# Feed-forward in eighths of a group, with the down product formed unit tile by unit tile

## The chip, the cores and the metric

The kernel runs on one core of a Trainium2 chip. The metric is the device time of one execution in microseconds; the time before is the median of three runs.

## The reference

Input is `x` of 64 batches with 256 tokens of 256 features, and `adj`, a 0/1 matrix for each batch. Two layers follow one another: each adds a graph part and then a feed-forward part to `x`, each behind a layer norm. The first layer's feed-forward is an LSTM of 256 steps. Only the last part, the second layer's feed-forward, is touched by the change:

```python
def blk_fn(xx):                                   # max-plus product, then two envelopes of 8 lines
    t = jnp.max(xx[:, None, :] + Wt[None, :, :], axis=-1) + bt
    z = t[:, :, None]
    cvx = jnp.max(z * sl_cvx[None] + of_cvx[None], axis=-1)
    ccv = jnp.min(z * sl_ccv[None] + of_ccv[None], axis=-1)
    return s * cvx + (1.0 - s) * ccv
trop = jax.lax.map(blk_fn, xb).reshape(T, FFN)
classical = jax.nn.gelu(xf @ Wc + bc, approximate=False)
g = jax.nn.sigmoid(xf @ Wg + bg)
fused = g * trop + (1.0 - g) * classical
out = fused @ Wd + bd
```

There are 16384 tokens, 256 features (`D`) and 1024 units (`FFN`, `FF`).

## The kernel before

A framework records the instructions and sets their order on each engine and the buffers of each pool at build time; within an engine the order is then fixed. `tc.issue_after(ins)` puts instructions behind another one on the same engine.

The kernel has stages in order of time: the first graph part, the LSTM, a short preparation, the second graph part, and from about 2660 us on the second feed-forward. The second graph part leaves for each token the normalised features, a copy in which only the features that can win the max-plus maximum stand, and the residual. It also leaves how many features can win.

The feed-forward sorts the tokens by that number in four blocks (`sorted_block`) and works on 128 tiles of 128 tokens, four tiles to a group (`GT` = 4), so 32 groups (`NGR`). Tiles at one place of a block take the same number of ranks, `RANKS`, from 40 down to 2; a group mixes tiles so that each has about the same sum. The 1024 units are 8 unit tiles (`NF` = 8), sorted by the number of hinges that their envelopes need, `HRANKS = [6, 3, 2, 2, 1, 1, 1, 0]`. A group passes through these pieces:

- `ask` (line 1274): GpSimd's indirect DMA gathers a tile's payload.
- `pick` (1282): VectorE finds the largest features, 8 at a time, with their numbers; TensorE transposes the tile and ScalarE copies it to `xr`.
- `maxplus` (1301): for each rank an indirect DMA of GpSimd brings one row of `wT_d` for each token (`row`, 128 x 1024, 10 buffers). The first rank of a tile goes through ScalarE (line 1313), which makes `acc`; all others are VectorE's step of line 1316, add and maximum.
- `classical` (1318): TensorE forms the gate and the GELU products of two unit tiles (line 1331), ScalarE applies the functions (line 1338), with a table load between the two.
- `fuse` (1340): TensorE transposes `acc` into `pa` (line 1348), ScalarE and VectorE form the hinges from it (`fused_hinges`, lines 1193 to 1203), and the result is a part of `fu`, which holds all 8 unit tiles of the group.
- `down` (1358): with the whole `fu` there, TensorE forms the down product in `po` for two tiles at a time (lines 1209 and 1211: the bias as a matmul of one row, then 8 products for each tile), and VectorE adds it to the residual (line 1218).
- `ask_rest` (1353) and `give_back` (1366): GpSimd gathers the residual and scatters the output.

The loop of line 1385 interleaves the pieces of neighbouring groups in quarters: while group g takes its rows, g - 1 is fused, g + 1 is asked for and picked, and g - 2 gets its down product. GpSimd's queue carries all indirect DMAs in this order; SP's and ScalarE's queues carry none in the group loop.

Of the kernel before, what the change touches and what calls it, by code (L numbers as in the profile page):

```python
# [2 lines left out]

# [6 lines left out]
F32 = mybir.dt.float32  # L10
# [5 lines left out]
AF = mybir.ActivationFunctionType  # L16
ALU = mybir.AluOpType
# [4 lines left out]
P = 128  # L22
# [35 lines left out]
def kernel(ctx: ExitStack, tc: tile.TileContext, a: dict, out: bass.AP):  # L58
# [16 lines left out]
    nc = tc.nc  # L75
    B, N, D = a["x"].shape
    H = D
    K = D // P
    NC = N // P
    FF = a["Wt"].shape[0]  # L80
    NF = FF // P
# [7 lines left out]
    ident = const.tile([P, P], F32, name="ident")  # L89
# [8 lines left out]
    ones = const.tile([P, N], F32, name="ones")  # L98
# [200 lines left out]
    with tc.tile_pool(name="b0", bufs=1) as wp:  # L299
        bias = wp.tile([6, 4 * P], F32, name="bias")  # L300
        part = wp.tile([6, 4 * P], F32, name="part")
# [220 lines left out]
    with (  # L522
# [345 lines left out]
        for k in range(HINGES):  # L868
            sc, of, sg = (prm_u[:, :, 4 + 3 * k + n] for n in range(3))
# [235 lines left out]
    CH = 512  # L1105
# [3 lines left out]
    class FeedForward:  # L1109
# [80 lines left out]
        def fused_hinges(self, f, pa, cl, gg, out, tag):  # L1190

            v = self.p4.tile([P, CH], F32, name=f"v_{tag}_{f}", tag="cvx")
            nc.scalar.activation(  # L1193
                v, pa, AF.Identity, bias=prm[:, f, 1:2], scale=prm[:, f, 0:1]
            )
            for k in range(HRANKS[f]):
                sc, of, sg = (prm[:, f, 4 + 3 * k + n : 5 + 3 * k + n] for n in range(3))
                u = self.u4.tile([P, CH], F32, name=f"u_{tag}_{f}_{k}", tag="u")
                nc.scalar.activation(u, pa, AF.Relu, bias=of, scale=sc)  # L1199
                nc.vector.scalar_tensor_tensor(v, u, sg, v, ALU.mult, ALU.add)  # L1200
            nc.vector.tensor_tensor(v, v, cl, ALU.subtract)
            nc.vector.tensor_tensor(v, v, gg, ALU.mult)  # L1202
            nc.vector.tensor_tensor(out, v, cl, ALU.add)  # L1203

        def down(self, fused, res, tag):

            po = self.ps_o.tile([P, NC, D], F32, name=f"po_{tag}", tag="po")
            for c in range(NC):
                nc.tensor.matmul(po[:, c, :], ones[0:1, :P], self.b_d, start=True, stop=False)
                for f in range(NF):  # L1210
                    nc.tensor.matmul(  # L1211
                        po[:, c, :],
                        fused(f, c),
                        self.w_d[:, f, :],
                        start=False,
                        stop=(f == NF - 1),
                    )
                nc.vector.tensor_tensor(res[c], res[c], po[:, c, :], ALU.add)

    with (  # L1220
        tc.tile_pool(name="w4", bufs=1) as wp,
        tc.tile_pool(name="s4", bufs=1) as sp,
        tc.tile_pool(name="pay4", bufs=5) as payp,
        tc.tile_pool(name="xr4", bufs=3) as xrp,
        tc.tile_pool(name="res4", bufs=7) as resp,
        tc.tile_pool(name="tk4", bufs=8) as tkp,
        tc.tile_pool(name="row4", bufs=10) as rowp,
        tc.tile_pool(name="acc4", bufs=8) as accp,
        tc.tile_pool(name="p4", bufs=2) as p4,
        tc.tile_pool(name="u4", bufs=3) as u4,  # L1230
        tc.tile_pool(name="cg4", bufs=2) as cgp,
        tc.tile_pool(name="fu4", bufs=1) as fup,
        tc.tile_pool(name="ps_c4", bufs=6, space=PSUM) as ps_c,
        tc.tile_pool(name="ps_o4", bufs=2, space=PSUM) as ps_o,
    ):
# [12 lines left out]
            nc.vector.tensor_copy(perm[blk][:, 1, :], order)  # L1248

        ff = FeedForward(wp, (p4, u4, cgp, ps_c, ps_o), True)  # L1250

        def place(i, of):
            j = i % NB
            return bass.IndirectOffsetOnAxis(ap=perm[i // NB][:, of, j : j + 1], axis=0)


        GT = CH // P
# [6 lines left out]
        class Group:  # L1264


            def __init__(self, g):
                self.g = g
                blk, m = divmod(g, GPB)
                self.tiles = [blk * NB + j for j in mixed[m]]  # L1270
                self.pay, self.val, self.num, self.acc, self.res = {}, {}, {}, {}, {}
                self.ranks = [(q, r) for q, i in enumerate(self.tiles) for r in range(RANKS[i % NB])]

            def ask(self, q):
# [26 lines left out]
            def maxplus(self, part):  # L1301

                n = len(self.ranks)
                for q, r in self.ranks[part * n // GT : (part + 1) * n // GT]:
                    i = self.tiles[q]
                    row = rowp.tile([P, FF], F32, name=f"row_{i}_{r}", tag="row")
                    nc.gpsimd.indirect_dma_start(  # L1307
                        row, None, wT_d, bass.IndirectOffsetOnAxis(ap=self.num[q][:, r : r + 1], axis=0)
                    )
                    v = self.val[q][:, r : r + 1]  # L1310
                    if r == 0:
                        acc = self.acc[q] = accp.tile([P, FF], F32, name=f"acc_{i}", tag="acc")
                        nc.scalar.activation(acc, row, AF.Identity, bias=v)  # L1313
                    else:
                        acc = self.acc[q]
                        nc.vector.scalar_tensor_tensor(acc, row, v, acc, ALU.add, ALU.max)  # L1316

            def classical(self, part):

                self.cg = {}  # L1320
                kinds = [
                    ("cl", ff.w_c, ff.col["bc"], AF.Gelu),
                    ("gg", ff.w_gt, ff.col["bg"], AF.Sigmoid),
                ]
                for n, wgt, bias, func in kinds[:: -1 if part % 2 else 1]:
                    res = self.cg[n] = cgp.tile([P, FQ, CH], F32, name=f"{n}_{self.g}_{part}", tag=n)
                    for e in range(FQ):
                        f = part * FQ + e
                        pc = ps_c.tile([P, CH], F32, name=f"pc_{n}_{self.g}_{f}", tag="pc")
                        for k in range(K):  # L1330
                            nc.tensor.matmul(  # L1331
                                pc,
                                wgt[:, k, f * P : (f + 1) * P],
                                self.xr[:, k, :],
                                start=(k == 0),
                                stop=(k == K - 1),
                            )
                        nc.scalar.activation(res[:, e, :], pc, func, bias=bias[:, f : f + 1])  # L1338

            def fuse(self, part):  # L1340
                g = self.g
                if part == 0:
                    self.fu = fup.tile([P, NF, CH], F32, name=f"fu_{g}", tag="fu")
                for e in range(FQ):
                    f = part * FQ + e
                    pa = ps_c.tile([P, CH], F32, name=f"pa_{g}_{f}", tag="pc")
                    for q in range(GT):
                        nc.tensor.transpose(  # L1348
                            pa[:, q * P : (q + 1) * P], self.acc[q][:, f * P : (f + 1) * P], ident
                        )  # L1350
                    ff.fused_hinges(f, pa, self.cg["cl"][:, e, :], self.cg["gg"][:, e, :], self.fu[:, f, :], g)

            def ask_rest(self, q):
                i = self.tiles[q]
                res = self.res[q] = resp.tile([P, D], F32, name=f"res_{i}", tag="res")
                nc.gpsimd.indirect_dma_start(res, None, res_d[i // NB], place(i, 0))

            def down(self, part):
                q0 = part * NC
                ff.down(  # L1360
                    lambda f, c: self.fu[:, f, (q0 + c) * P : (q0 + c + 1) * P],
                    [self.res[q0 + c] for c in range(NC)],
                    f"{self.g}_{part}",
                )

            def give_back(self, q):
                nc.gpsimd.indirect_dma_start(  # L1367
# [5 lines left out]
        FQ = NF // GT  # L1373
        NGR = NT // GT
        groups = [Group(g) for g in range(NGR)]

        def each(g, piece, *args):
            if 0 <= g < NGR:
                getattr(groups[g], piece)(*args)
# [3 lines left out]
            groups[0].ask(q)  # L1383
            groups[0].pick(q)
        for g in range(NGR + 2):
            for q in range(GT):
                if q == 0:
                    for part in range(GT // NC):
                        each(g - 2, "down", part)
                    each(g - 1, "classical", 0)  # L1390
                each(g + 1, "ask", q)
                each(g, "maxplus", q)
                each(g - 1, "fuse", q)
                if q + 1 < GT:
                    each(g - 1, "classical", q + 1)
                each(g + 1, "pick", q)
                each(g - 1, "ask_rest", q)
                each(g - 2, "give_back", q)
            if g % GPB == GPB - 2 and g + 2 < NGR:
                sorted_block((g + 2) // GPB)  # L1400

# [19 lines left out]
    with tc.If(bad > 0):  # L1421
        with (
# [9 lines left out]
            ff = FeedForward(wp, (p4, u4, cgp, ps_c, ps_o), False)  # L1432
# [6 lines left out]
            with tc.For_i(0, NBLK, 1) as blk:  # L1439

                acc = [accp.tile([P, TOK], F32, name=f"accg{f}", tag=f"acc{f}") for f in range(NF)]
# [26 lines left out]
                for ch in range(NCH):  # L1468
# [3 lines left out]
                    cl, gg = ff.classical(xr, f"g{ch}")  # L1472
# [83 lines left out]
```

## Time and profile before

| | us |
|---|---|
| median of three runs (5421.66 to 5444.79) | 5427.94 |
| profiled execution, time | 5416.64 |
| profiled execution, span | 5414.8 |
| feed-forward, group loop (2690 to 5350) | 2660 |
| VectorE busy in it | 2315.19 |
| GpSimd busy in it | 1917.03 |
| ScalarE busy in it | 1263.52 |
| TensorE busy in it | 1819.53 |

A page of a profile shows one execution. It has the busy time of each engine, the span in 40 slices with a digit for the busy share of each, the groups of instructions by line (count, busy time, mean of one, idle time before them and what ended it), and the DMA issues. DVE is VectorE, ACT is ScalarE, POOL is GpSimd, PE is TensorE. The issuing of an instruction by GpSimd's sequencer is not counted as busy. Where a wait's releaser is "remote" or "issue", the trace names no instruction that ended it.

### The profile page before, as it was taken

The page shows a single profiled execution, that of the slowest core. Times are in us where ns is not written, and L with a number is a line of the kernel's source. Part 1 is how long each engine was busy: PE and PEld are TensorE (multiplying, and loading weights), DVE is VectorE, ACT ScalarE, POOL GpSimd, SP SyncE. Part 2 cuts the span into 40 slices and gives each one's busy share as a digit, 9 for nine tenths or more (in the row PEclk, how much of TensorE's full clock was granted, in tenths as well). Part 3 has the DMA queues.
Part 4 walks back from the last instruction along what each step waited for, and adds up shares of the span by engine and source line. Part 5 has one row for each costly group of instructions (what it writes and reads, how often), then busy time and mean ns, then how long its engine had stood idle before and what let it go on. Part 6 is the DMA issues. An engine that isn't in the chain of part 4 may idle for free. (4 is left out here: it accounts for less than half of the span.)

```text
span 5414.8 us, 58603 instructions
## 1 busy us (share of the span) xinstructions
PE 4203.9 (78%) x17787; PEld 2348.7 (43%) x17788; DVE 4183.2 (77%) x9223; ACT 2276.6 (42%) x4245; POOL 2546.2 (47%) x2739
## 2 busy tenths in 40 slices
PE   6999979999999978888547677577675776666777
PEld 4666623333333336666424334344343443334444
DVE  5777776555555568888788799888898888897997
ACT  2555512222222225555434444354444544345555
POOL 1333310000000025555488667777667676677764
PEclk8999989999999989999768888788887888888889
DMA  4322212111111124444388776777767777677774
GB/s 107 94 84 85 72 38 73 46 28 28 28 28 28 28 83 143 143 138 139 131 301 270 258 252 229 262 250 264 251 231 261 252 270 248 220 259 261 268 258 140
DMA packets 454032, 886.60 MB, mean 164 GB/s; under 512 B 60232, under 2 KB 285004, under 8 KB 453708
## 3 DMA queue, kind: packets, MB, share of 16 engines
q0 software_dynamic: 192448, 685.96, 37.9%
q1 hardware_dynamic: 253476, 193.64, 12.5%
q10 hardware_dynamic: 7784, 3.17, 0.3%
q8 instruction: 143, 2.34, 0.2%
q14 instruction: 181, 1.48, 0.1%
HBM read 773.34 MB, written 110.26 MB: 163 GB/s over the span
## 5 line engine op out<-in xcount | busy, mean ns | idle before, releaser
L1307 POOL DMA_INDIRECT row<-wT_d,num x1172 | 1421.4, 1213 | 565.6 <-issue 277.9
L1316 DVE SCALAR_TENSOR_TENSOR acc<-row,val,acc 128x1024 f32<-128x1024 f32 x1044 | 1314.1, 1279 | 166.0 <-DMA row<-wT_d,num 161.3
L1211 PE MATMUL po<-w_d,fu 128*128 128x256 f32 x2048 | 593.5, 436 | 106.8 <-DVE fu L1203 100.0
L1331 PE MATMUL pc_gg<-xr,w_gt 128*128 128x512 f32 x1024 | 538.0, 667 | 97.2 <-ACT u L1199 64.2
L568 PE MATMUL pg<-w_hh,hT 128*64 128x512 f32 x2040 | 501.5, 613 | 91.6 <-DVE hT L695 91.5
L949 POOL TENSOR_TENSOR adjT<-adjT,ident 128x128 f32<-128x128 f32 x128 | 61.5, 502 | 1020.3 <-PE pg L568 991.6
L1211 PEld LDWEIGHTS po<-w_d,fu 128*128 128x128 f32 x2048 | 422.2, 218 | 266.7 <-DVE fu L1203 147.9
L1331 PE MATMUL pc_cl<-xr,w_c 128*128 128x512 f32 x1024 | 491.5, 621 | 23.8 <-issue 11.9
L568 PE MATMUL pg<-w_ih,XT 128*64 128x512 f32 x2048 | 486.9, 597 | 3.3 <-DMA w_ih<-in_W_ihT_dram 3.3
L1199 ACT ACTIVATE u<-pa,prm 128x512 f32<-128x512 f32 x512 | 383.0, 778 | 248.0 <-DVE v L1200 203.3
L1313 ACT ACTIVATE acc<-row,val 128x1024 f32<-128x1024 f32 x128 | 146.9, 1148 | 751.1 <-DMA row<-wT_d,num 751.1
L675 ACT ACTIVATE sg<-pg 128x256 f32<-128x256 f32 x256 | 98.1, 383 | 839.0 <-PE pg L568 832.3
L1200 DVE SCALAR_TENSOR_TENSOR v<-u,prm,v 128x512 f32<-128x512 f32 x512 | 376.1, 747 | 49.4 <-ACT u L1199 48.7
L1348 PE MATMUL pa<-ident,acc 128*128 128x128 f32 x1024 | 195.1, 326 | 262.7 <-ACT u L1199 82.9
L1331 PEld LDWEIGHTS pc_gg<-xr,w_gt 128*128 128x128 f32 x1024 | 209.4, 213 | 357.8 <-issue 208.9
L1331 PEld LDWEIGHTS pc_cl<-xr,w_c 128*128 128x128 f32 x1024 | 201.1, 202 | 256.5 <-issue 225.5
L173 DVE TENSOR_SCALAR xn<-x,mv,rstd 128x256 f32<-128x256 f32 x512 | 207.1, 426 | 135.6 <-POOL rstd L166 126.6
L1348 PEld LDWEIGHTS pa<-ident,acc 128*128 128x128 f32 x1024 | 146.3, 167 | 335.9 <-issue 113.0
L568 PEld LDWEIGHTS pg<-w_ih,XT 128*64 128x64 f32 x2048 | 148.9, 139 | 301.8 <-issue 301.8
L681 DVE TENSOR_TENSOR cc<-sg,cc 128x128 f32<-128x128 f32 x255 | 74.5, 292 | 261.5 <-ACT sg L675 260.3
L1193 ACT ACTIVATE v<-pa,prm 128x512 f32<-128x512 f32 x256 | 198.9, 777 | 168.1 <-DVE fu L1203 146.4
L1338 ACT ACT_TABLE_LOAD x201 | 257.9, 1283 | 18.6 <-DVE v L1202 12.2
(391 smaller groups left out, 8114.5 us busy)
## 6 DMA issues: line engine op xcount, KB each, us to landing
adjT<-in_adjT_dram SPq DMA_DIRECT2D x128, 256.0 KB, 2.7
row<-wT_d,num POOLq DMA_INDIRECT x1172
x<-in_x_dram SPq DMA_DIRECT2D x64, 256.0 KB, 2.8
x_d<-x SPq DMA_DIRECT2D x64, 256.0 KB, 2.5
x1s<-x_d SPq DMA_DIRECT2D x128, 128.0 KB, 2.9
x_d<-x1s SPq DMA_DIRECT2D x128, 128.0 KB, 2.5
x<-x_d SPq DMA_DIRECT2D x64, 256.0 KB
res_d<-x SPq DMA_DIRECT2D x64, 256.0 KB, 2.7
```

Source lines behind the costliest of these rows:

```text
L173: nc.vector.tensor_scalar(xn[:, c, :], x[:, c, :], mv[:, c, 0:1], rstd[:, c : c + 1], ALU.subtract, ALU.mult)
L568: ins = nc.tensor.matmul(half(pg, j), by(k), gates_of(w, k, j), start=False, stop=(last and k == K - 1), tile_position=(0, j * B),)
L1193: nc.scalar.activation(v, pa, AF.Identity, bias=prm[:, f, 1:2], scale=prm[:, f, 0:1])
L1199: nc.scalar.activation(u, pa, AF.Relu, bias=of, scale=sc)
L1200: nc.vector.scalar_tensor_tensor(v, u, sg, v, ALU.mult, ALU.add)
L1211: nc.tensor.matmul(po[:, c, :], fused(f, c), self.w_d[:, f, :], start=False, stop=(f == NF - 1),)
L1307: nc.gpsimd.indirect_dma_start(row, None, wT_d, bass.IndirectOffsetOnAxis(ap=self.num[q][:, r : r + 1], axis=0))
L1313: nc.scalar.activation(acc, row, AF.Identity, bias=v)
L1316: nc.vector.scalar_tensor_tensor(acc, row, v, acc, ALU.add, ALU.max)
L1331: nc.tensor.matmul(pc, wgt[:, k, f * P : (f + 1) * P], self.xr[:, k, :], start=(k == 0), stop=(k == K - 1),)
L1338: nc.scalar.activation(res[:, e, :], pc, func, bias=bias[:, f : f + 1])
L1348: nc.tensor.transpose(pa[:, q * P : (q + 1) * P], self.acc[q][:, f * P : (f + 1) * P], ident)
```

## The change

The loop over quarters of a group becomes one over its 8 unit tiles. `maxplus` takes an eighth of the ranks at a time, and `fuse` makes one unit tile in a buffer of its own (3 buffers of 128 x 512 instead of one of 128 x 8 x 512). `down` now takes one unit tile: right after it is fused, four products (one for each tile of the group) add to the two accumulators `po`, which stay open for the whole group and begin with a bias product of 512 columns from `b_d2`, a row that holds the bias twice. The residual is added by `add_rest` in the next group's first four eighths. A tile's `pick` comes one quarter later. ScalarE's first rows are recorded with `issue_after`, behind the last activation of the unit tile fused before. The pools grow: payload 5 to 6, residual 7 to 8, rows 10 to 13, hinge inputs 3 to 4.

```diff
-            nc.scalar.activation(
+            last = nc.scalar.activation(
                 v, pa, AF.Identity, bias=prm[:, f, 1:2], scale=prm[:, f, 0:1]
             )
...
-                nc.scalar.activation(u, pa, AF.Relu, bias=of, scale=sc)
+                last = nc.scalar.activation(u, pa, AF.Relu, bias=of, scale=sc)
...
             nc.vector.tensor_tensor(out, v, cl, ALU.add)
+            return last
...
-        tc.tile_pool(name="pay4", bufs=5) as payp,
+        tc.tile_pool(name="pay4", bufs=6) as payp,
...
-        tc.tile_pool(name="res4", bufs=7) as resp,
+        tc.tile_pool(name="res4", bufs=8) as resp,
...
-        tc.tile_pool(name="row4", bufs=10) as rowp,
+        tc.tile_pool(name="row4", bufs=13) as rowp,
...
-        tc.tile_pool(name="u4", bufs=3) as u4,
+        tc.tile_pool(name="u4", bufs=4) as u4,
...
-        tc.tile_pool(name="fu4", bufs=1) as fup,
+        tc.tile_pool(name="fu4", bufs=3) as fup,
...
+        b_d2 = wp.tile([1, NC, D], F32, name="b_d2")
+        for c in range(NC):
+            nc.scalar.dma_start(b_d2[:, c, :], a["bd"].unsqueeze(0))
...
-                for q, r in self.ranks[part * n // GT : (part + 1) * n // GT]:
+                for q, r in self.ranks[part * n // NF : (part + 1) * n // NF]:
...
                         acc = self.acc[q] = accp.tile([P, FF], F32, name=f"acc_{i}", tag="acc")
-                        nc.scalar.activation(acc, row, AF.Identity, bias=v)
+                        with tc.issue_after(last_act.ins) if last_act else nullcontext():
+                            nc.scalar.activation(acc, row, AF.Identity, bias=v)
...
-            def fuse(self, part):
-                g = self.g
-                if part == 0:
-                    self.fu = fup.tile([P, NF, CH], F32, name=f"fu_{g}", tag="fu")
-                for e in range(FQ):
-                    f = part * FQ + e
-                    pa = ps_c.tile([P, CH], F32, name=f"pa_{g}_{f}", tag="pc")
-                    for q in range(GT):
-                        nc.tensor.transpose(
-                            pa[:, q * P : (q + 1) * P], self.acc[q][:, f * P : (f + 1) * P], ident
-                        )
-                    ff.fused_hinges(f, pa, self.cg["cl"][:, e, :], self.cg["gg"][:, e, :], self.fu[:, f, :], g)
+                self.cgs.append(cg)
+
+            def fuse(self, f):
+                nonlocal last_act
+                g, e = self.g, f % FQ
+                pa = ps_c.tile([P, CH], F32, name=f"pa_{g}_{f}", tag="pc")
+                for q in range(GT):
+                    nc.tensor.transpose(
+                        pa[:, q * P : (q + 1) * P], self.acc[q][:, f * P : (f + 1) * P], ident
+                    )
+                self.fu = fup.tile([P, CH], F32, name=f"fu_{g}_{f}", tag="fu")
+                last_act = ff.fused_hinges(f, pa, self.cgs[f // FQ]["cl"][:, e, :], self.cgs[f // FQ]["gg"][:, e, :], self.fu, g)
...
-            def down(self, part):
-                q0 = part * NC
-                ff.down(
-                    lambda f, c: self.fu[:, f, (q0 + c) * P : (q0 + c + 1) * P],
-                    [self.res[q0 + c] for c in range(NC)],
-                    f"{self.g}_{part}",
-                )
+            def down(self, f):
+
+                if f == 0:
+                    self.po = [
+                        ps_o.tile([P, NC, D], F32, name=f"po_{self.g}_{i}", tag="po") for i in range(GT // NC)
+                    ]
+                    for po in self.po:
+                        nc.tensor.matmul(po, ones[0:1, :P], b_d2, start=True, stop=False)
+                for q in range(GT):
+                    po = self.po[q // NC][:, q % NC, :]
+                    nc.tensor.matmul(
+                        po, self.fu[:, q * P : (q + 1) * P], ff.w_d[:, f, :], start=False, stop=(f == NF - 1 and q % NC == NC - 1)
+                    )
+
+            def add_rest(self, q):
+                res = self.res[q]
+                nc.vector.tensor_tensor(res, res, self.po[q // NC][:, q % NC, :], ALU.add)
...
-            for q in range(GT):
-                if q == 0:
-                    for part in range(GT // NC):
-                        each(g - 2, "down", part)
+            for f in range(NF):
+                q, e = divmod(f, FQ)
+                if f == 0:
+                    each(g - 2, "down", NF - 1)
                     each(g - 1, "classical", 0)
-                each(g + 1, "ask", q)
-                each(g, "maxplus", q)
-                each(g - 1, "fuse", q)
-                if q + 1 < GT:
+                else:
+                    each(g - 1, "down", f - 1)
+                if e == 0:
+                    each(g + 1, "ask", q)
+                each(g, "maxplus", f)
+                if f < GT:
+                    each(g - 2, "add_rest", f)
+                each(g - 1, "fuse", f)
+                if e == 0 and q + 1 < GT:
                     each(g - 1, "classical", q + 1)
-                each(g + 1, "pick", q)
-                each(g - 1, "ask_rest", q)
-                each(g - 2, "give_back", q)
+                if e == 1:
+                    if q > 0:
+                        each(g + 1, "pick", q - 1)
+                    each(g - 1, "ask_rest", q)
+                    each(g - 2, "give_back", q)
+            each(g + 1, "pick", GT - 1)
```

More of the change, by code (lines that the diff above doesn't have):

```diff
@@ L1 @@
 import math
-from contextlib import ExitStack
+from contextlib import ExitStack, nullcontext
 import concourse.bass as bass
@@ L1271, in __init__ @@
                 self.pay, self.val, self.num, self.acc, self.res = {}, {}, {}, {}, {}
+                self.cgs = []
                 self.ranks = [(q, r) for q, i in enumerate(self.tiles) for r in range(RANKS[i % NB])]
@@ L1318, in classical @@
             def classical(self, part):
-                self.cg = {}
+                cg = {}
                 kinds = [
@@ L1325, in classical @@
                 for n, wgt, bias, func in kinds[:: -1 if part % 2 else 1]:
-                    res = self.cg[n] = cgp.tile([P, FQ, CH], F32, name=f"{n}_{self.g}_{part}", tag=n)
+                    res = cg[n] = cgp.tile([P, FQ, CH], F32, name=f"{n}_{self.g}_{part}", tag=n)
                     for e in range(FQ):
@@ L1375 @@
         groups = [Group(g) for g in range(NGR)]
+        last_act = None
         def each(g, piece, *args):
```

## The prediction

> **What bounds the kernel now.** I read the page first: engine shares, then the slices.
>
> ```profile
> span 5414.8 us, 58603 instructions
> PE 4203.9 (78%) x17787; PEld 2348.7 (43%) x17788; DVE 4183.2 (77%) x9223; ACT 2276.6 (42%) x4245; POOL 2546.2 (47%) x2739
> ...
> DVE  5777776555555568888788799888898888897997
> ACT  2555512222222225555434444354444544345555
> POOL 1333310000000025555488667777667676677764
> ```
>
> VectorE's second half is a plateau at 8 and 9 of 10, beside a GpSimd at 6 to 8. That is the feed-forward, the only stage that the change touches. The busy time by stage gives its sizes:
>
> ```profile
> 2690.00:5350.00 2660.00, 1819.53 (x5551) 1029.15 (x5552) 2315.19 (x3223) 1263.52 (x1694) 1917.03 (x1545) 0.82 0.77 256
> 5350.00:5415.00 65.00, 51.79 (x194) 32.78 (x192) 39.49 (x61) 31.86 (x44) 9.54 (x9) 0.94 0.07 24
> ```
>
> The columns after the width are PE, PE loads, VectorE, ScalarE, GpSimd, granted clock, DMA share, GB/s. VectorE works 2315 of 2660 us. GpSimd shows 1917, but each of its 1545 instructions is preceded by 0.30 us of issue: 1917 + 464 = 2381. So two engines are 87 and 90% full and neither is the bound alone: each waits for the other in turn. Who waits for whom (total us, times, longest), in the same window:
>
> ```profile
> DVE acc L1316 <- DMA row<-wT_d,num: 161.3, 60, 10.3
> DVE res L1218 <- remote: 51.6, 12, 6.3
> DVE v L1200 <- ACT u L1199: 46.8, 12, 9.4
> DVE val L1290 <- DMA pay<-pay_d,perm: 32.8, 5, 11.0
> DVE res L1218 <- PE po L1211: 28.7, 23, 5.3
> DVE res L1218 <- PE pa L1348: 13.2, 4, 4.8
> ...
> POOL row L1307 <- ACT acc L1313: 165.2, 67, 5.9
> ...
> ACT acc L1313 <- DMA row<-wT_d,num: 751.1, 107, 33.2
> ```
>
> VectorE's waits sum to 346 us: rows 161, the residual adds on the down product 100 (with 6.7 of issue), hinge inputs from ScalarE 47, payloads 33. GpSimd's largest is ScalarE's first rows. ScalarE stands 751 us before a first row that has not landed, with everything queued behind. One stall in order of time:
>
> ```profile
> 4103.20 1.28 DVE L1316 SCALAR_TENSOR_TENSOR acc<-row,val,acc 128x1024 f32<-128x1024 f32 x1 [0.51 <-DMA row<-wT_d,num]
> 4114.74 7.53 DVE L1316 SCALAR_TENSOR_TENSOR acc<-row,val,acc 128x1024 f32<-128x1024 f32 x6 [10.26 <-DMA row<-wT_d,num]
> ...
> 4113.40 1.15 ACT L1313 ACTIVATE acc<-row,val 128x1024 f32<-128x1024 f32 x1 [12.72 <-DMA row<-wT_d,num]
> ...
> 4114.81 0.94 POOL L1307 DMA_INDIRECT row<-wT_d,num  x1 [3.31 <-ACT acc L1313]
> ```
>
> In the built program VectorE's order puts row 1 of a new tile ahead of five rows of the old one, but GpSimd issues those five first. Row 0 left at 4106.85, ScalarE got it at 4113.40, and VectorE stood 10.26 us though its own next row needed less. GpSimd then stood 3.31 us for a buffer that ScalarE held. It is the order and the buffers, not the amount of work, that costs here. The prices of one row, from the groups (mean in ns after the comma):
>
> ```profile
> L1307 POOL DMA_INDIRECT row<-wT_d,num x1172 | 1421.4, 1213 | 565.6 <-issue 277.9
> L1316 DVE SCALAR_TENSOR_TENSOR acc<-row,val,acc 128x1024 f32<-128x1024 f32 x1044 | 1314.1, 1279 | 166.0 <-DMA row<-wT_d,num 161.3
> ```
>
> GpSimd spends 1.21 + 0.30 us on a row and VectorE 1.28, so GpSimd can't make up for a late start.
>
> **The change part by part.** The orders of the two built programs are compared engine by engine.
>
> *Rows: smaller pieces, first rows behind the hinges, 13 buffers.* Counts of rows are unchanged (1172 issues, 1044 VectorE steps, 128 ScalarE). I counted, per VectorE step, how many unused rows GpSimd must have issued up to the needed one. Before, 118 of 1044 steps ask for 3 to 8; after, 23 ask for 3 or 4. I also counted how many row issues lie between a buffer's use and its reuse. Before, 91 of 128 first-row buffers come back within 5 issues, so GpSimd must wait for a row it has just sent; after, 9, and most at 6 to 13. GpSimd's wait for ScalarE: 165 us, of which 67 x 0.3 is plain issue, so 145; I leave 20 and take 125. VectorE's row waits: 161, about 11 of them in the first 75 us, when nothing is buffered. New is that a group's first row now stands on ScalarE behind gate work: between it and the first row before it lie three table loads and five activations, some 8 us, against some 7 us of VectorE steps. That is about 1 us in each of 32 groups, between nothing, if ScalarE runs ahead, and 3 us each. I leave 60 in all and take 90. Waits on hinge inputs (47): the long ones, 9.4, 8.1 and 8.6, follow a ScalarE standing before a row; I take 30.
>
> *Down product by unit tile.* Each unit tile now gives four products at once, and VectorE adds the residual in the next group. That removes most of the 100 us: after the last product, the order leaves one to twelve VectorE steps in front of the first add, so I leave 20 and take 80. Matmuls stay 2048. Bias matmuls go from 256 recorded of 256 columns (0.456 us each, 117) to 128 of 512, which by the gate product's row of that width take some 0.65, 83. The 34 us leave an engine with 840 us idle: nothing, as VectorE and GpSimd cover it. The new wait: every product waits for its unit's last VectorE step, and the transposes and gate products queued behind it wait too. In the order the transposes run 3 unit tiles ahead in 168 of 256 cases, 2 in 61, so I price it at nothing; a gain has no reason, and the other end is the loss of the third rival. Three buffers of fused rows make VectorE's last step wait for the product three units back; same cover. Two extra bias loads of 1 KB on ScalarE's queue land before the first group's end.
>
> *GpSimd's queue.* Asks, residual loads and scatters move past rows by eighths but stay the same 3 x 128; scatters waiting for a residual add cost 26.5 us, minus 10 x 0.3; I take 15. At the block borders the new order has the maxima directly behind the new permutation as before, so the payload waits (33) and GpSimd's wait for the numbers (13) stay. Deeper pools for payload and residual remove small waits; nothing.
>
> *ScalarE's table loads.* The program's loads rise from 213 to 259. The trace's row is 1283 ns (257.9 us for 201), and the next activation starts 1.30 us after a load starts (4004.13, then 4005.43): 46 x 1.30 = 60 us. The Trainium skill, "ScalarE: Activation LUTs", section "What ACT_TABLE_LOAD costs", speaks against the change: with a drain every switch takes about 2.66 us, so 46 cost 122 us. No drain shows here, so I take 60. ScalarE has 1396 us idle in the stage; both are hidden unless ScalarE is what the others wait for.
>
> *The tail.* After the last fused tile (5391.7) the kernel now runs some 40 recorded matmuls and VectorE waits 1.7 + 4.7 + 4.4 us for them; the new order has four products (8 recorded) left. I take 10.
>
> **The sum**, from both ends. VectorE: 90 + 80 + 30 + 10 = 210. GpSimd: 125 + 15 + 15 (its waits for other ScalarE steps, 10.6 and 8.9, and a few for VectorE) + 10 = 165. Both have to hold, so the smaller, 165, counts: the rest of VectorE's gain turns into waiting for GpSimd. One price more: with less VectorE idle time GpSimd's issues lengthen. In the stall above they took 0.93 and 0.94 us, a little earlier, beside VectorE's two-input steps, 1.49; the mean is 1.213. The Trainium skill, "SBUF — State Buffer", section "SBUF: two separate sides", makes this a lock: an operation of VectorE that takes the shared port blocks GpSimd in full. By it each of some 90 issues that now fall into idle time would wait for a whole step, 1.3 us: 117 us. By the rows they go from 0.94 to 1.21: 25, and half of these stalls stay: 12. The trace wins. 165 − 12 = 153. Against the profiled execution, 5416.6 us (span 5414.8), that is 5263.6; the median of the runs, 5427.9, lies 11.3 higher, so the forecast is 5275.
>
> **The rivals.** *All waits go.* GpSimd's 2381 us become the stage, plus 25 for longer issues and 20 of waits at the block borders, 2426: a gain of 234 and the tail's 10, so 5184. For: the counts above nearly vanish. Against: GpSimd 99% and VectorE 95% full would need more slack than 13 rows give.
>
> *The waits move.* GpSimd runs into VectorE as its releaser instead of ScalarE, and VectorE waits for first rows that ScalarE now takes later, behind table loads. Then half of the adds' gain (40), the tail (10) and a little of the rows (10) are left, 60: 5368. For: GpSimd's pace is set by one queue in order. Against: its waits for VectorE are 39 us now, of which 58 x 0.3 is issue.
>
> *Slower: TensorE becomes the bound.* A product per unit tile stands in TensorE's queue until VectorE has finished that unit. TensorE has 840 us idle per 256 units, 3.3 us each. A wait of that kind is 146 / 75 = 1.9 us now. If every unit had one, and it were 3.9 us, the stage would grow by 256 x 0.6 = 154 us: 5582. It decides from 3.3. Against: the transposes stand mostly three units ahead.
>
> That the change does not do what it says is excluded by the orders.
>
> **How the numbers follow.** Forecast, 5215 to 5330: 0.55. All waits go, below 5215: 0.15. Waits move, 5330 to 5400: 0.13. Within 0.5% (27 us, about what a measurement of this kernel can tell from no change): 0.05. Slower by TensorE: 0.12. So faster 0.83. The range runs from 5165 to 5430: below lie some 0.05, above half of "within" and the slower case, 0.15.
>
> **What would show it.** Right: VectorE's plateau at 9; its waits for rows near 70 us, for residual adds near 20; GpSimd's waits for first rows near 20, ScalarE's 751 much lower; table loads near 247 (201 recorded of 213, the rest in a branch not taken, and 46). Wrong: GpSimd's waits for VectorE in place of ScalarE (second rival), TensorE waiting for the fused tile hundreds of us and VectorE's hinge steps for ScalarE (third), or issues longer than 1.3 us.

## The result, and the profile after

The changed kernel takes 5434.97 us (median of 12 runs, 5422.63 to 5442.74), beside 5428.74 us of the kernel before in the same comparison (12 runs). The ratio is 1.0017, 95% interval 1.0004 to 1.0029. So a forecast gain of 153 us came out as no gain, if anything as a loss of 9 us. GpSimd's waits did go; something of the same size came in their place.

The page of the changed kernel, to be laid beside the lines of before:

```profile
span 5433.5 us, 58722 instructions
...
PE 4217.1 (78%) x17659; PEld 2337.9 (43%) x17660; DVE 4180.9 (77%) x9223; ACT 2337.4 (43%) x4291; POOL 2715.2 (50%) x2739
...
DVE  5777776555555568888788988889888888888986
...
POOL 1333310000000035555488876777767887677874
```

VectorE's plateau is no higher than it was: 8 more often than 9. VectorE's total is the same, 4181 against 4183 us. The total that has changed is GpSimd's: 2715 against 2546 us, for the same 2739 instructions. The same shows by stage (columns: stretch and width, then PE, PE loads, VectorE, ScalarE, GpSimd, granted clock, DMA share, GB/s):

```profile
2690.00:5350.00 2660.00, 1828.28 (x5426) 1018.21 (x5427) 2302.38 (x3198) 1315.95 (x1730) 2071.62 (x1534) 0.80 0.77 254
5350.00:5440.00 90.00, 54.82 (x184) 33.32 (x182) 45.02 (x67) 38.82 (x50) 18.50 (x16) 0.85 0.18 60
```

GpSimd went from 1917 us in 1545 instructions to 2072 us in 1534. With 0.305 us of issue ahead of each it is now 2072 + 468 = 2540 of 2660 us, 95%, where the prediction had 90%. The waits in that stretch (us in total, times, longest), VectorE's first:

```profile
DVE acc L1323 <- DMA row<-wT_d,num: 133.8, 113, 5.6
DVE val L1295 <- DMA pay<-pay_d,perm: 60.0, 3, 20.6
DVE v L1200 <- ACT u L1199: 56.1, 17, 9.8
DVE fu L1203 <- PE po L1374: 34.3, 11, 5.2
DVE res L1380 <- PE po L1374: 18.7, 6, 4.7
DVE res L1380 <- issue: 17.7, 3, 6.6
...
POOL res L1362 <- DMA out_dram<-res,perm: 54.6, 37, 4.2
POOL row L1312 <- ACT acc L1320: 52.3, 7, 13.7
...
ACT acc L1320 <- DMA row<-wT_d,num: 675.2, 89, 25.4
```

GpSimd's wait for ScalarE's first rows fell from 165 to 52 us, 67 times to 7. VectorE's longest wait for a row fell from 10.3 to 5.6 us, but it now waits 113 times instead of 60: many short waits in place of a few long ones, which fits an engine that another one paces. The groups say what GpSimd does instead of waiting (mean ns after the comma):

```profile
L1312 POOL DMA_INDIRECT row<-wT_d,num x1172 | 1567.3, 1337 | 421.7 <-issue 278.2
L1323 DVE SCALAR_TENSOR_TENSOR acc<-row,val,acc 128x1024 f32<-128x1024 f32 x1044 | 1333.1, 1281 | 158.2 <-DMA row<-wT_d,num 137.2
```

The 1172 row issues fetch what they fetched before, but one now takes 1.337 us instead of 1.213. VectorE's step is the same to 2 ns.

**GpSimd's ledger.** I add up GpSimd's queue in each trace from the first indirect DMA of the feed-forward to the end of the last: their durations, 0.305 us of issue ahead of each of 1556, and what is left between them, the waits.

| us | instructions | issue | waits | length | mean row issue |
|---|---|---|---|---|---|
| before | 1929 | 474 | 317 | 2721 | 1.213 |
| changed | 2097 | 474 | 174 | 2745 | 1.337 |

Waits 143 less, instructions 168 more. The rest of the study asks what lengthened an issue, and whether GpSimd really is the bound.

**What an issue waits for.** One stretch of the changed kernel in order of time (start, duration), VectorE and then GpSimd:

```profile
4023.40 1.28 DVE L1323 SCALAR_TENSOR_TENSOR acc<-row,val,acc 128x1024 f32<-128x1024 f32 x1
4024.60 0.68 DVE L1202 TENSOR_TENSOR v<-v,gg 128x512 f32<-128x512 f32 x1
4025.20 1.28 DVE L1323 SCALAR_TENSOR_TENSOR acc<-row,val,acc 128x1024 f32<-128x1024 f32 x1
4026.39 0.68 DVE L1203 TENSOR_TENSOR fu<-v,cl 128x512 f32<-128x512 f32 x1
4027.00 1.28 DVE L1323 SCALAR_TENSOR_TENSOR acc<-row,val,acc 128x1024 f32<-128x1024 f32 x1
...
4024.60 1.49 POOL L1312 DMA_INDIRECT row<-wT_d,num  x1 [0.30 <-issue]
4026.40 1.49 POOL L1312 DMA_INDIRECT row<-wT_d,num  x1 [0.31 <-issue]
```

And one of the kernel before, where VectorE has eight row steps in a row:

```profile
4440.94 9.92 DVE L1316 SCALAR_TENSOR_TENSOR acc<-row,val,acc 128x1024 f32<-128x1024 f32 x8
...
4442.13 0.94 POOL L1307 DMA_INDIRECT row<-wT_d,num  x1 [0.30 <-issue]
4443.37 0.93 POOL L1307 DMA_INDIRECT row<-wT_d,num  x1 [0.30 <-issue]
...
4447.11 0.94 POOL L1307 DMA_INDIRECT row<-wT_d,num  x1 [0.30 <-DVE acc L1316]
4448.36 0.94 POOL L1307 DMA_INDIRECT row<-wT_d,num  x1 [0.30 <-issue]
```

In the first, the issue at 4024.60 begins together with a hinge step, which ends at 4025.28; 0.81 us later, at 4026.09, the issue is done. Its 0.305 us of issue later the next one begins, at 4026.40, just as the next hinge step begins at 4026.39, and pays again. Row step and hinge step together take 1.80 us, and so does 1.49 + 0.305: the two queues lock, one issue to each pair. In the second, 0.94 + 0.305 = 1.245 us is almost the pace of the row steps. Each issue goes ahead, and VectorE's steps come 9.92 / 8 = 1.24 us apart, where the row step above is followed after 1.20. Same instructions, and the length of an issue depends on which step of VectorE it meets and where in that step it falls.

Which step it meets shows best where the two begin together. Three steps and three issues of the kernel before, from the stretch that the prediction quoted its 1.49 from:

```profile
4087.43 0.69 DVE L1202 TENSOR_TENSOR v<-v,gg 128x512 f32<-128x512 f32 x1
4089.23 0.69 DVE L1203 TENSOR_TENSOR fu<-v,cl 128x512 f32<-128x512 f32 x1
4091.02 0.75 DVE L1200 SCALAR_TENSOR_TENSOR v<-u,prm,v 128x512 f32<-128x512 f32 x1
...
4087.44 1.49 POOL L1307 DMA_INDIRECT row<-wT_d,num  x1 [0.30 <-issue]
4089.24 1.49 POOL L1307 DMA_INDIRECT row<-wT_d,num  x1 [0.30 <-issue]
4091.03 0.93 POOL L1307 DMA_INDIRECT row<-wT_d,num  x1 [0.30 <-issue]
```

Each issue begins 0.01 us after a step. Behind the two `TENSOR_TENSOR` steps it waits; beside the `SCALAR_TENSOR_TENSOR` step it goes ahead.

The row issues of both traces follow one pattern. The port here is the access to SBUF that the two engines share. If it is free, an issue takes 0.94 us. If a row step or hinge step is running, it takes the rest of that step plus 0.81 us (in the changed kernel the duration less the rest of the step lies between 0.809 and 0.815 for the middle half of these issues). In some it loses to the next step too and takes 2.1 us. Where an issue starts within 0.08 us of a step's start, the operation decides: beside `SCALAR_TENSOR_TENSOR` (row steps and the hinge steps of line 1200) 202 of 209 go ahead free before and 50 of 55 in the changed kernel; beside `TENSOR_TENSOR` (the other hinge steps, 0.68 us) 42 of 45 wait before and 165 of 169 in the changed kernel. Why the two operations differ is open. Beside a residual add (one operand in PSUM) or the maxima (one operand) it doesn't wait: 94 such issues in the changed kernel have 0.01 us of excess over 0.94. Counted (between 2700 and 5340 us of the trace):

| issues that | before | changed |
|---|---|---|
| find no such step, or one that ends within some 0.13 us | 370 | 324 |
| go ahead beside one | 204 | 64 |
| wait for one step | 545 | 686 |
| wait for two | 44 | 83 |
| excess over 0.94, us | 318 | 459 |

What the eighths did to VectorE's order explains the counts. In the traces a row step stands directly between two hinge steps of the 0.68 us kind 103 times before and 328 times in the changed kernel (the expectations below give 131 and 393, from the built orders); row steps in runs of four or more were 34% and are 6%. So 169 issues instead of 45 begin together with a `TENSOR_TENSOR` step. The excess over 0.94 us of issues that start beside such steps went from 45 to 111 us, and beside the `SCALAR_TENSOR_TENSOR` steps from 265 to 338.

### The profile page after: what moved, and what is told of

The parts are those of the page before. It is cut to its first block, busy times and chain, and to the rows that moved or that the text cites. A ratio compares the mean times of both kernels' runs of the same rounds, so it can differ in the third digit from the quotient of the medians.

```text
span 5433.5 us, 58722 instructions
## 1 busy us (share of the span) xinstructions
PE 4217.1 (78%) x17659; PEld 2337.9 (43%) x17660; DVE 4180.9 (77%) x9223; ACT 2337.4 (43%) x4291; POOL 2715.2 (50%) x2739
## 5 line engine op out<-in xcount | busy, mean ns | idle before, releaser
L1312 POOL DMA_INDIRECT row<-wT_d,num x1172 | 1567.3, 1337 | 421.7 <-issue 278.2
L1323 DVE SCALAR_TENSOR_TENSOR acc<-row,val,acc 128x1024 f32<-128x1024 f32 x1044 | 1333.1, 1281 | 158.2 <-DMA row<-wT_d,num 137.2
L1338 PE MATMUL pc_gg<-xr,w_gt 128*128 128x512 f32 x1024 | 561.4, 696 | 119.7 <-ACT gg L1345 76.8
L1338 PEld LDWEIGHTS pc_gg<-xr,w_gt 128*128 128x128 f32 x1024 | 227.4, 228 | 390.9 <-issue 230.3
L1345 ACT ACT_TABLE_LOAD x247 | 316.9, 1283 | 19.6 <-DVE v L1202 15.3
```

Of the source, the lines that this page charges most:

```text
L1312: nc.gpsimd.indirect_dma_start(row, None, wT_d, bass.IndirectOffsetOnAxis(ap=self.num[q][:, r : r + 1], axis=0))
L1338: nc.tensor.matmul(pc, wgt[:, k, f * P : (f + 1) * P], self.xr[:, k, :], start=(k == 0), stop=(k == K - 1),)
```

## The experiments

Theory A: GpSimd is the bound, and its row issues lengthen because the finer pieces alternate row and hinge steps on VectorE. Theory B: more rows in flight lengthen the issues. Theory C: GpSimd is not the bound, and new waits in the other queues gave the gain back. Ratios are to the kernel before, each with its own runs on the same chip; what is said against the changed kernel is the difference of two ratios times 5429 us. A fourth cause can be set aside with the runs: TensorE's granted clock was 0.80 in the stage against 0.82 before, but the times don't follow it. It is 0.82 and 0.83 in e1 and e7, which are not faster than the kernel before, and 0.81 in e9, which is 1.5% faster.

**The hinge tile in PSUM, changed kernel (e1).**

```diff
-            v = self.p4.tile([P, CH], F32, name=f"v_{tag}_{f}", tag="cvx")
+            v = self.ps_c.tile([P, CH], F32, name=f"v_{tag}_{f}", tag="pc")
```

> The changed kernel with one edit: the hinge tile v lies in PSUM (in the rotation of the six gate banks) instead of SBUF, so that VectorE's five hinge steps of a unit read one SBUF operand instead of two. Theory A (GpSimd has become the bound, and a row issue that starts while a VectorE step with two SBUF operands runs has to wait for that step's end, then takes 0.81 us more; beside steps with one SBUF or a PSUM operand it takes 0.94): the excess over 0.94 us of issues that start beside hinge steps, 131 us in the changed kernel's trace, goes to near 0, and part of the 323 us beside row steps goes too where a hinge step followed; mean row issue from 1.34 to 1.10 to 1.22; time 80 to 150 us less. Theory B (more rows in flight lengthen the issues in the queues): mean stays 1.31 to 1.37, time within 20 us. Theory C (GpSimd is not the bound, the gain was given back by new waits of VectorE and TensorE): the issues may shorten, but the time falls by less than 40 us. Four tiles instead of three per unit turn in six banks, which could cost up to 50 us by any theory.

Ratio 1.0111 (1.0096 to 1.0126), 51 us over the changed kernel: A's time is a miss, and C's mark, a fall of less than 40 us, came. What it says of the issue held. Hinge steps and issues in one stretch of this kernel:

```profile
2864.58 0.74 DVE L1200 SCALAR_TENSOR_TENSOR v<-u,prm,v 128x512 f32<-128x512 f32 x1
2865.23 0.68 DVE L1202 TENSOR_TENSOR v<-v,gg 128x512 f32<-128x512 f32 x1
2865.84 0.74 DVE L1200 SCALAR_TENSOR_TENSOR v<-u,prm,v 128x512 f32<-128x512 f32 x1
2866.49 0.68 DVE L1203 TENSOR_TENSOR fu<-v,cl 128x512 f32<-128x512 f32 x1
...
2864.18 0.94 POOL L1312 DMA_INDIRECT row<-wT_d,num  x1 [0.30 <-issue]
2865.43 0.94 POOL L1312 DMA_INDIRECT row<-wT_d,num  x1 [0.31 <-issue]
2866.68 0.94 POOL L1312 DMA_INDIRECT row<-wT_d,num  x1 [0.30 <-issue]
```

The issue at 2865.43 begins with 0.48 us of a hinge step to go and takes 0.94. Issues that begin with 0.25 to 0.5 us of a hinge step of the 0.68 us kind left and take under 0.96 are 77 here and none in the changed kernel. The excess beside hinge steps, 131 us in the changed kernel, is about 1 us here. So it is the second SBUF operand that holds an issue up (line 1203 still writes to SBUF, and the issue at 2866.68 goes ahead beside it). The mean fell to 1.265 only, because issues that no longer waited for hinge steps ran into row steps: their excess rose from 319 to 351 us. And the waits came back, in the ledger from 174 to 321 us. TensorE now stands for a bank (0.9 us for this releaser in the changed kernel), and GpSimd's residual gathers stand 140 us for scatters instead of 55; that the first brought the second is argued:

```profile
PE pc_cl L1338 <- ACT v L1193: 209.7, 23, 17.3
```

**The same edit in the kernel before (e2).**

> The same edit in the kernel before: v in PSUM. Its issues that start beside hinge steps have 77 us of excess. A: this goes, and the mean row issue falls from 1.21 to about 1.13; but GpSimd there stands 269 us in waits for others as well, so the time falls only by 20 to 80 us, less than in the changed kernel. B: issues and time unchanged. C: issues shorter, time within 20 us.

Ratio 0.9962 (0.9948 to 0.9975), 21 us less, at the low end of A; C's "within 20 us" is not told apart from it. The row issue falls from 1.213 to 1.163 us, and GpSimd's waits rise from 317 to 359 us:

```profile
L1307 POOL DMA_INDIRECT row<-wT_d,num x1172 | 1363.3, 1163 | 554.6 <-issue 269.0 <-ACT acc L1313 188.5 <-DVE acc L1316 26.3
```

**Ten row buffers in the changed kernel (e3).** `bufs=13` becomes `bufs=10` in the pool `row4`.

> The changed kernel with 10 row buffers instead of 13. A: rows in flight do not lengthen an issue; the mean stays 1.28 to 1.37, GpSimd's waits for buffers grow from about 120 us, and the time is 10 to 70 us longer. B: the issues fall back towards the 1.21 of before (under 1.26), time within 20 us or shorter. C: no clear change of either.

Ratio 1.0104 (1.0085 to 1.0123), 47 us over the changed kernel. The mean issue is 1.303, not near 1.21, and the waits in the ledger rise from 174 to 210 us. B falls: fewer rows in flight barely shorten an issue, and the three buffers are worth having.

**No residual gather on GpSimd (e4).** The residual then belongs to other rows.

```diff
-                nc.gpsimd.indirect_dma_start(res, None, res_d[i // NB], place(i, 0))
+                nc.sync.dma_start(res, res_d[i // NB][(i % NB) * P : (i % NB + 1) * P, :])
```

> The changed kernel, but the residual rows are read in unsorted order by a plain DMA on SyncE's queue, so that the residual added belongs to other rows: this leaves the gather of the residual (128 indirect DMAs) out of GpSimd's queue. A (GpSimd is the bound at 95 per cent): 128 x (1.34 + 0.30) = 210 us of its work and up to 55 us of its waits for the scatters' buffers go; VectorE has some 350 us idle, so the time falls by 120 to 210 us. C (not the bound): the time falls by less than 50 us. B makes no difference to A here.

Ratio 0.972 (0.9698 to 0.9741), 161 us less than the changed kernel. Taking 128 instructions out of GpSimd's queue moves the end; VectorE's work is the same. In the ledger 106 us of instructions, 39 of issue and 46 of waits go. The gathers' own 172 us were more, but the row issues that are left lengthen again, from 1.337 to 1.404 us. GpSimd paces the changed kernel, and C falls as the main cause.

**Rows by quarters in the changed kernel (e5).** Only the pieces of rows are undone.

```diff
-                each(g, "maxplus", f)
+                if e == 0:
+                    each(g, "maxplus", f)
+                    each(g, "maxplus", f + 1)
```

> The changed kernel with one part undone: both eighths of rows of a quarter are given out together, ahead of the quarter's first unit tile, as before; hinges and down product stay unit tile by unit tile. In the built order of VectorE a row step stands alone between two hinge steps that take SBUF operands alone 393 times in the changed kernel, 131 before, 197 here; 7, 35 and 29 per cent of the row steps stand in runs of four or more. Theory A (a row issue waits for VectorE steps with two SBUF operands; in a run of row steps it falls into step with them and begins just behind a step's start, where it goes ahead free; in the alternation of row step and hinge step it begins half a step in and loses to the hinge step too): issues that go ahead free beside a running step go up from 64 towards the 204 of before, the mean issue falls from 1.34 to 1.20 to 1.27, GpSimd's busy time by 80 to 150 us. Time 20 to 100 us less than the changed kernel, if its waits stay away; if the pieces had also taken the waits away, up to 30 us more. Theory C (waits and order of the other queues gave the gain back): issues change by less than 0.03 and the time stays within 20 us.

Ratio 0.9819 (0.9794 to 0.9845): 5316.56 us, faster than both kernels, 107 us less than the changed one. The row group (between 2690 and 5350 us):

```profile
L1312 POOL DMA_INDIRECT row<-wT_d,num x1166 | 1466.4, 1258 | 421.0 <-issue 260.1 <-ACT acc L1320 59.0 <-DMA row<-wT_d,num 31.7
```

and VectorE's slices on the page:

```profile
DVE  5777767555555558888788989889999899998997
```

The issue is back at 1.26, 130 issues go ahead free (64 in the changed kernel), and in the ledger the instructions take 1981 us with the waits as low as in the changed kernel, 173. VectorE now has the plateau of 9 that the prediction looked for. The stage is 117 us shorter, of which 116 is instruction length.

**Eighths of rows in the kernel before (e6).** Rows in `NF` pieces instead of `GT`, one ahead of each unit tile's hinges; nothing else.

> The kernel before with that part alone: rows in eighths, one ahead of each unit tile's hinges; down product, first rows, buffers as before. The alternation stands 374 times in VectorE's built order (131 before). A: the mean issue rises from 1.21 to 1.28 to 1.36 with nothing else changed, free ones beside a running step fall from 204 to below 110; GpSimd's busy time rises by 70 to 150 us, and as its waits are still there, the time rises by 0 to 80 us. C: issues within 0.03 of 1.21, and the time falls or stays.

Ratio 1.0058 (1.0036 to 1.0079), 31 us more. The ledger shows both effects of this one part: waits from 317 to 207 us, instructions from 1929 to 2072. The row issue (between 2690 and 5350 us):

```profile
L1307 POOL DMA_INDIRECT row<-wT_d,num x1157 | 1519.1, 1313 | 455.3 <-issue 237.1 <-ACT acc L1313 77.6 <-DVE val L1290 29.6
```

Free ones beside a step are 107. So this part alone brings 110 us and costs 143.

**The hinge tile in place (e7).** It takes the bank of the transposed tile, so three tiles a unit turn in six banks as in the changed kernel.

```diff
-            v = self.p4.tile([P, CH], F32, name=f"v_{tag}_{f}", tag="cvx")
...
+            v, us = pa, []
...
-        tc.tile_pool(name="u4", bufs=4) as u4,
+        tc.tile_pool(name="u4", bufs=6) as u4,
```

> The changed kernel with the hinge tile v written in place over the transposed tile in PSUM, after the unit's Relu tiles (six of these instead of four; the two SBUF buffers of v go). VectorE's hinge steps then have one SBUF operand as with v in a bank of its own, but three tiles per unit turn in the six banks as in the changed kernel. A: issues beside hinge steps go ahead free; mean issue 1.20 to 1.28; GpSimd's busy time falls by 80 to 150 us, and without the price of the banks the time falls by 40 to 120 us against the changed kernel. If instead v in PSUM is what cost the 51 us there (and not the banks), the time stays 20 to 60 us above it. Each pa bank is held about 3 us longer, until the third hinge step, which may cost up to 40 us.

Ratio 1.0026 (1.0007 to 1.0045), the changed kernel's time within 5 us: a miss on time, a hit on the issue (1.249) and on instructions (2097 to 1966 us). The waits ate all of it, 174 to 293 us. VectorE's residual adds and GpSimd's residual gathers:

```profile
DVE res L1382 <- PE po L1376: 193.0, 26, 14.1
...
POOL res L1364 <- DMA out_dram<-res,perm: 112.7, 59, 4.6
```

The products come late, so the adds, so the scatters, and the gather behind a scatter waits for its buffer. That a bank held longer makes the products late is argued, not isolated.

**First rows not placed (e8).** The `issue_after` is left out of the changed kernel.

> The changed kernel without the rule that places ScalarE's first rows behind the last hinge activation given out. The alternation stands 347 times. A: the issues stay long, 1.30 to 1.36; GpSimd waits for ScalarE's first rows again as before (165 us against 52), so the time is 20 to 110 us longer. C: if that rule is what gave the gain back (first rows late for VectorE, table loads), the time is 20 us or more shorter.

Ratio 1.016 (1.0134 to 1.0186), 78 us over the changed kernel. Issues stay long (1.321) and the ledger's waits rise to 274 us. The rule is worth what it costs; ScalarE's order did not give the gain back. GpSimd's wait for first rows rose only to 84 us, less than the 165 expected; ScalarE's own wait before such rows rose from 675 to 956 us, and VectorE's for hinge inputs from 56 to 156.

**Rows by halves (e9).** As e5, with four eighths together.

> The changed kernel with the rows of four eighths given out together, ahead of the first and the fifth unit tile of a group: one step further than quarters. In VectorE's built order row steps between two hinge steps stand alone 211 times (197 with quarters, 393 in the changed kernel), and 39 per cent of the row steps are in runs of four or more (29 with quarters, 7). Theory A (the pattern of row and hinge steps on VectorE sets the length of a row issue): mean issue 1.20 to 1.27, like the 1.26 of the quarters; the coarser pieces bring back waits for buffers and first rows, so the time is 0 to 80 us over that of the quarters. A rival (any coarser giving out is better, by the queues' order alone): again 50 us or more less than the quarters.

Ratio 0.9848 (0.9831 to 0.9866), 16 us over the quarters in the difference of the ratios. The intervals overlap, so the two are not told apart; but 50 us less, the mark of "any coarser giving out is better", did not come. The issue is 1.264, as the lone row steps would have it (165 in this trace, 162 with quarters), and VectorE's waits for rows are 198 us against 145.

**Quarters and the tile in place (e10).**

> Both edits together: rows by quarters, and the hinge tile written in place over the transposed tile in PSUM. A: mean issue falls below either alone (1.26 and 1.25), to 1.13 to 1.21. If GpSimd is still the bound, the time falls by 30 to 80 us against the quarters alone; if the bank that is held longer delays the products and so the residual adds, the scatters and the gathers behind them, as it did without the quarters (VectorE stood 193 us for products at the residual add, GpSimd 113 us at the residual gather), the gain is eaten again and the time is within 30 us of the quarters or over it.

Ratio 0.9825 (0.9798 to 0.9851), no different from the quarters alone:

```profile
L1314 POOL DMA_INDIRECT row<-wT_d,num x1171 | 1384.1, 1182 | 467.0 <-issue 243.1 <-ACT acc L1322 76.9 <-DVE acc L1325 39.8
```

The issues shorten as expected, below either edit alone, and GpSimd's instructions to 1882 us; the waits rise from 173 to 279. The two effects cancel here as well. So e1, e7 and e10 shorten the issues without shortening the kernel: other waits take the room. Only where the waits stayed as they were (e5 and e9 against the changed kernel) did the time fall as far as the issues did, and there the order of the rows was changed, not the place of an operand.

## Why the prediction was wrong, point by point

*What failed* is the price of "GpSimd's issues lengthen", 12 us. It was written for "some 90 issues that now fall into idle time", by the rows from 0.94 to 1.21 us. Measured: all 1556 instructions changed their place beside VectorE's steps, and together they cost 168 us more. Two errors are in that step. I took a mean of 1.21 as the price "beside VectorE", where the trace held two prices, 0.94 and the rest of a step plus 0.81; the 1.49 that I had quoted stood beside `TENSOR_TENSOR` steps, a 0.93 of the same stretch beside a `SCALAR_TENSOR_TENSOR` step. And I counted issues that move into idle time, not those that stay and meet another order. I had compared VectorE's two orders for which row is asked when, and not for which step stands next to which.

*The rule that I set aside* had the kind right. The Trainium skill, "SBUF — State Buffer", section "SBUF: two separate sides", says that a VectorE operation with two SBUF inputs and a GpSimd operation that reads SBUF exclude each other: whichever starts first has the shared port for its whole length. The runs agree in this: with one operand in PSUM the issues beside the hinge steps are free (excess 1 us in e1, none in e10, against 131). Its 117 us, for 90 issues, would have made the sum 165 − 117 = 48 and the forecast 5380, still a gain. The trace adds what such an estimate lacks: of the issues that begin together with a step, those beside `SCALAR_TENSOR_TENSOR` go ahead and those beside `TENSOR_TENSOR` wait, so the cost depends on which steps the queue falls in with.

*GpSimd's account of waits*, 165 us, was right in size: 143 in the changed kernel and 144 in e5. Its largest term, the first rows, came to 165 − 52 = 113 us of the 125. Scatters behind late adds became gathers behind scatters (13.9 us before, 54.6 now), which was priced at nothing ("remove small waits; nothing"). With the waits' 144 us less 51 of longer instructions e5 gets 93 us of stage and 98 us of time: the sum works once the issue is priced.

*VectorE's account*, 210 us, can't be had while GpSimd is the bound. Its row waits were to fall to 70 and are 134; hinge inputs were to fall by 30 and went from 47 to 56; residual adds fell from 100 to 44 us (with 7.5 behind another matmul) instead of 20. The three buffers of fused rows, "same cover", cost 34 us of waits at line 1203. The payload waits that were to stay went from 33 to 60. With VectorE idle for 358 us in the stage and GpSimd full to 95%, none of them decided the time.

*Table loads*: 247 recorded, as foretold, at 1283 ns each.

*The rivals.* "All waits go" had named GpSimd as the next bound and was right there, but priced longer issues at 25 us. "The waits move" to VectorE as releaser did not come: 16 us. "TensorE becomes the bound" did not come: its wait for the fused tile is 146.0 us in 77 times, 1.9 us each, far from the 3.9 for every unit. The mark set for being wrong, "issues longer than 1.3 us", is what happened.

## What to carry to other kernels

When GpSimd issues many indirect DMAs beside a busy VectorE, look at the distribution of the issue's duration and not its mean: the difference between the shortest and the rest was, here, time lost to VectorE's steps with two SBUF operands, and it belongs in the sum for any edit that reorders VectorE. Cutting work into finer pieces removes waits and at the same time alternates the steps; find the piece size by both (here quarters, not eighths, with the other parts of the change kept: 1.8% faster than before; halves, 1.5%, are not told apart from them). A wait removed from the engine that is the bound is only gained if its own instructions stay as long, and shorter instructions are only gained if no other wait takes their place.

## What the runs showed of the hardware

- An indirect DMA of 128 rows took GpSimd 0.94 us, or the rest of VectorE's running step plus 0.81 us if that step read two SBUF operands. A step with one operand, or one of two in PSUM, didn't hold it up (0.01 us of excess in 94 issues).
- Where an issue began within 0.08 us of a step's start, it went ahead of 252 of 264 `SCALAR_TENSOR_TENSOR` steps and waited for 207 of 214 `TENSOR_TENSOR` steps (both kernels together). An issue that waited for two steps took some 2.1 us.
- In the run of 1.28 us row steps that is shown the two queues fell into step at 1.24 us for a step and an issue; in the alternation with 0.68 us steps they locked at 1.80 us for two steps and one issue.
- GpSimd's queue with few waits left VectorE idle for 358 us in 2660. The pacing engine's busy row showed 78% only, since 0.305 us of issue per instruction isn't counted as busy.
